# Output projection in four parts between attention steps, and bias adds moved behind the latest exp

## The chip, the cores and the metric

The kernel runs on one core of a Trainium2 chip. The core has engines with an instruction queue each: TensorE (PE, matrix products into PSUM), VectorE (DVE), ScalarE (ACT), GpSimd (POOL) and SyncE (SP, which issues the DMAs). Instructions of one engine run in their order; an instruction that needs another engine's result waits on a semaphore, and everything behind it in its queue waits too. The metric is the device time in microseconds, the median of several runs.

## The reference

Four layers on x of shape (4, 512, 32, 32) in float32, with 1024 tokens in each of four batches:

```
layer 0: attention, 8 heads of 64:   x = softmax(q k / 8) v @ Wo + bo + x
layer 1: linear attention:           x = x + gamma * wval(x)
layer 2: layer norm, one head of 512, x = x + out
layer 3: group norm, 4 heads of 128: x = x + proj(softmax(q k / sqrt(128)) v)
```

The change lies in the attention of layers 0 and 3, and in the code that forms q and k.

## The kernel before

Tokens are handled in two blocks of 512 (qb), channels in four chunks of 128 (g or o). `attention` serves layers 0 and 3. It goes through steps (qb, g, i). `scores` forms one product of keys and queries into a two-bank PSUM tile and takes its exp on ACT (L917) into a tile pt, which DVE adds to a running sum (L921, L924). `values` multiplies pt with v two steps later (L936 in layer 0, L951 in layer 3). In layer 0 a head is 64 wide and a chunk holds a pair of heads: the products there use 64 x 64 parts of the array, with four products to a step, and the loop takes two steps at a time (`per` is 2). In layer 3 a head is a chunk, products are 128 x 128, and `per` is 1.

When a chunk's steps are done, `sum_rows` (L963 or L971, and in layer 0 a copy on ACT at L968 and an add on DVE at L969) and `invert` (a reciprocal, L673, and two maxima, L675 and L676) give the softmax's divisor. `normalise` multiplies (L980) and adds the output bias to x in place, on ACT (L982).

When all four chunks of a block are done, `project_out` multiplies the attention's output (the tile ot) with the output weights. It uses seven products on 2 x 2 blocks in place of eight: product 1 in two halves, then 6, 7 and 5, then the second halves of 7 and 5, each of four matmuls of 128 x 256 (L1012). DVE forms the sums of inputs (`sum_inputs`, L681 to L684) and adds the results into x (L1020, L1041). The function is in two parts: `lead` holds the first half of product 1, a copy on ACT (L1032) and the input sums; `rest` holds all else. In layer 3 each finished piece is sent out by a DMA on SP (L1025). The fourth block of layer 0's last batch goes through `project_out_plain`, and the last block of layer 3 through `end_program`.

PSUM has four one-bank tiles (acc), which values, row sums, projections and the products of q and k share, and two two-bank tiles (sc), which scores use.

The order on PE is written out by hand (`manual_schedule`). Work that is to come later stands in a list, `later`, with a count that `tick` lowers; `tick` is called after each `values`, and an entry runs when its count is spent. The last block of a batch has its projection left in `later` when the next batch begins; there `seven_products`, which forms q and k, takes entries from the list between its first eight products (p1 and p2, L701): one after the fifth, all that is left after the sixth. Other engines' orders come from a scheduler that builds the program; `issue_after(ins)` holds the instructions traced inside it behind `ins` in their engine's queue.

Between the batches of layer 0, `pieces` of layer 1 for the batch before run in `slot`: the first, `gates`, takes a maximum over x on DVE (L1217) and four row sums on ACT (L1220).

Of the kernel before, what the change touches and what calls it, by code (L numbers as in the profile page):

```python
# [14 lines left out]
AF = mybir.ActivationFunctionType  # L15
# [459 lines left out]
def plain_path(ctx: ExitStack, tc: tile.TileContext, d: dict, out: bass.AP, count):  # L475
# [178 lines left out]
    def slot():  # L654
        tick()
        if pieces:
            pieces.pop(0)()
# [47 lines left out]
    def seven_products(  # L705
        n, weights, inputs, bias, dst, sums, ws=None, matmul=tokens_moving, view=lambda ps: ps,
        slots=0, first=False, done=lambda tb, o: None,
    ):

        stt = nc.vector.scalar_tensor_tensor
        one, five, seven, made = {}, {}, {}, {}  # L720
        inner = lambda o: block_sums(lambda i, j: weights(i, j, o))

        def mult(o, ps, w, x, start=True, stop=True, ms=(0, 1)):
            for m in ms:
                matmul(ps, w, x, m, o, start and m == 0, stop and m == 1)

        def join(out, ps, i, o, other):

            if bias is None:
                nc.vector.tensor_tensor(out, view(ps), other, ALU.add)  # L730
            else:
                joined[:] = [stt(out, view(ps), bias(i, o), other, ALU.add, ALU.add).ins]

        def p1(o, ms=(0, 1)):
            if 0 in ms:
                one[o] = acc_tile()
            mult(o, one[o], weights(0, 0, o), inputs(0, 0), stop=False, ms=ms)
            if 1 in ms:
                nc.scalar.copy(dst(0, 1, o), view(one[o]))  # L739

        def p2(o, ms=(0, 1)):
            mult(o, one[o], weights(0, 1, o), inputs(1, 0), start=False, ms=ms)
            if 1 in ms and bias is None:
                nc.scalar.copy(dst(0, 0, o), view(one.pop(o)))
            elif 1 in ms:
                nc.scalar.activation(dst(0, 0, o), one.pop(o), AF.Identity, bias=bias(0, o))

        def p3(o):
            mult(o, five[o], made[o][3], inputs(1, 1), start=False)
            join(dst(0, 1, o), five.pop(o), 0, o, dst(0, 1, o))  # L750
            done(1, o)

        def p4(o):
            mult(o, seven[o], weights(1, 1, o), t[3], start=False)
            join(dst(1, 0, o), seven.pop(o), 1, o, dst(0, 1, o))
            done(0, o)

        def p5(o):
            five[o] = acc_tile()
            mult(o, five[o], made[o][0], t[0], stop=False)  # L760
            join(dst(1, 1, o), five[o], 1, o, dst(1, 1, o))

        def p6(o):
            ps = acc_tile()
            mult(o, ps, made[o][1], t[1])
            nc.vector.tensor_tensor(dst(0, 1, o), dst(0, 1, o), view(ps), ALU.add)

        def p7(o):
            seven[o] = acc_tile()
            mult(o, seven[o], made[o][2], t[2], stop=False)  # L770
            nc.vector.tensor_tensor(dst(1, 1, o), dst(0, 1, o), view(seven[o]), ALU.add)


        if first:
            for f in (p1, p2):
                for m in range(2):
                    for o in range(n):
                        f(o, (m,))
            for o in range(2):
                made[o] = inner(o)  # L780
            t = sums()
        else:
            calls = [(p1, 0), (p1, 1), (p2, 0), (p2, 1)]
            if n > 2:
                calls += [(p1, 2), (p1, 3), (p2, 2), (p2, 3)]
            for i, (f, o) in enumerate(calls):
                f(o)
                if i < 2:
                    made[o] = (ws or inner)(o)
                if i == 1:  # L790
                    tick()
                if i == 4 and later:
                    later.pop(0)[1]()
                if i == min(5, len(calls) - 1):
                    t = sums()
                    while later:
                        later.pop(0)[1]()
                if i % 2 and i // 2 >= len(calls) // 2 - slots:
                    slot()
        for a in range(0, n, 2):  # L800
            for o in (a, a + 1):
                if o not in made:
                    made[o] = (ws or inner)(o)
            order = [
                (p6, a), (p7, a), (p6, a + 1), (p5, a), (p4, a), (p7, a + 1), (p3, a), (p5, a + 1),
                (p4, a + 1), (p3, a + 1),
            ]
            for i, (f, o) in enumerate(order):
                f(o)
                if i % 2:  # L810
                    slot()
# [75 lines left out]
    def attention(b, q, key, v, heads, scale, wo, os, bo, hooks={}, last=False, end=None, plain=False):  # L887
# [9 lines left out]
        steps = [  # L897
            (qb, g, i) for qb in range(NTB) for g in range(NC) for i in range(nsteps)
        ]
        pts, accs, rds, outs, ots = {}, {}, {}, {}, {}  # L900
        half = lambda i: slice(i * P // 2, (i + 1) * P // 2)

        def scores(n):
            qb, g, i = steps[n]
            ps = two_tile("sc")
            if pair:
                for h, s in itertools.product(range(2), range(2)):
                    nc.tensor.matmul(  # L908
                        ps[half(h), s, :], lhsT=key(g, i)[half(s), half(h)],
                        rhs=q[qb][half(s), g, :], start=True, stop=True,  # L910
                    )
            for s in range(0 if pair else 2):
                nc.tensor.matmul(  # L913
                    ps[:, s, :], lhsT=key(g, 2 * i + s), rhs=q[qb][:, g, :], start=True, stop=True
                )
            pt = pt_tile("pt")
            nc.scalar.activation(pt, ps, AF.Exp, scale=scale)  # L917
            pts[n] = pt
            if i == 1:
                accs[qb, g] = acc = sum_tile("sum")  # L920
                nc.vector.tensor_tensor(acc, pts[n - 1], pt, ALU.add)  # L921
            elif i > 1:
                acc = accs[qb, g]
                nc.vector.tensor_tensor(acc, acc, pt, ALU.add)  # L924
            if i == nsteps - 1 and not pair:
                nc.vector.tensor_tensor(acc[:, 0, :], acc[:, 0, :], acc[:, 1, :], ALU.add)
# [48 lines left out]
        def normalise(qb, g):  # L975
            rd = rds.pop((qb, g))
            if g == 0 and not pair:
                ots[qb] = chunks_tile("ot", "ot")
            o = ots[qb][:, g, :]
            nc.vector.tensor_tensor(o, o if pair else outs.pop((qb, g))[0], rd, ALU.mult)  # L980
            xv = x[:, g, bass.ts(qb, TB)]
            nc.scalar.activation(xv, xv, AF.Identity, bias=bo[:, g : g + 1])  # L982

        def finish(qb, o, ps):
            xv = x[:, o, bass.ts(qb, TB)]
# [4 lines left out]
        def project_out(qb):  # L990
# [26 lines left out]
            def add(i, out, *others):  # L1017

                for a in (view(ps[i]), *others):
                    nc.vector.tensor_tensor(out, out, a, ALU.add)  # L1020
# [6 lines left out]
                        xv(i, tb),  # L1027
                    )

            def lead():  # L1030
                mult(1, w(0, 0), inputs(0, 0), stop=False)
                nc.scalar.copy(d, view(ps[1]))  # L1032
                sum_inputs(t, inputs)

            def rest():
                mult(1, w(0, 1), inputs(1, 0), start=False)
                finish(0, 0, 1, xv(0, 0))
                mult(6, os[1], t[1])
                add(6, d)
                mult(7, os[2], t[2], stop=False)  # L1040
                nc.vector.tensor_tensor(e, d, view(ps[7]), ALU.add)  # L1041
                mult(5, os[0], t[0], stop=False)
                finish(1, 1, 5, xv(1, 1), e)
                mult(7, w(1, 1), t[3], start=False)
                finish(1, 0, 7, xv(1, 0), d)
                mult(5, os[3], inputs(1, 1), start=False)
                finish(0, 1, 5, xv(0, 1), d)

            return lead, rest

        def start_out(qb, halves):
            halves.extend(project_out(qb))
            halves[0]()

        def project_out_plain(qb):
            ot = ots.pop(qb)
# [35 lines left out]
        for m in range(0, len(steps) + 2, per):  # L1092
# [3 lines left out]
            for n in range(m, m + per):  # L1096
                if n >= 2:
# [11 lines left out]
                    if n - 2 == len(steps) - 1 and end is not None:  # L1109
                        flush()  # L1110
                        end_program(qb)
                    elif final and g == NC - 1 and plain and qb == NTB - 1:
                        later.append([2 * per + 1, lambda qb=qb: project_out_plain(qb)])
                    elif final and g == NC - 1:
                        halves = []
                        later.append([2 * per, lambda qb=qb, p=halves: start_out(qb, p)])
                        later.append([2 * per + 1, lambda p=halves: p[1]()])
                if parts:
                    parts.pop(0)()
                if n in hooks:  # L1120
# [598 lines left out]
```

## Time and profile before

| what | value |
|---|---|
| median of 3 runs | 2520.86 us (2520.38 to 2520.89) |
| profiled execution | 2520.85 us |
| its span | 2518.9 us |
| mean granted TensorE clock | 0.999 |
| ACT busy in the span | 705.5 us (28%) |
| DVE busy in the span | 1608.0 us (64%) |

The profile is one execution. A line of the timeline has the start in us, the duration, the engine, the source line, the operation, the tile written and the tiles read with partitions and elements, the count merged into the line, and in brackets the idle time before it and what ended it. A matmul in float32 leaves two records, so "x8" stands for four matmuls. An ACT_TABLE_LOAD changes the set of functions that ACT can evaluate. The wait list gives, for an engine's line and what it waited for, the total in us, how often, and the longest.

### The profile page before, as it was taken

The page shows a single profiled execution, that of the slowest core. Times are in us where ns is not written, and L with a number is a line of the kernel's source. Part 1 is how long each engine was busy: PE and PEld are TensorE (multiplying, and loading weights), DVE is VectorE, ACT ScalarE, POOL GpSimd, SP SyncE. Part 2 cuts the span into 40 slices and gives each one's busy share as a digit, 9 for nine tenths or more (in the row PEclk, how much of TensorE's full clock was granted, in tenths as well). Part 3 has the DMA queues.
Part 4 walks back from the last instruction along what each step waited for, and adds up shares of the span by engine and source line. Part 5 has one row for each costly group of instructions (what it writes and reads, how often), then busy time and mean ns, then how long its engine had stood idle before and what let it go on. Part 6 is the DMA issues. An engine that isn't in the chain of part 4 may idle for free.

```text
span 2518.9 us, 24923 instructions
## 1 busy us (share of the span) xinstructions
PE 2488.8 (99%) x10266; PEld 1287.7 (51%) x10266; DVE 1608.0 (64%) x1815; ACT 705.5 (28%) x859; POOL 254.8 (10%) x240
## 2 busy tenths in 40 slices
PE   9999999999999999999999999999999999999999
PEld 4545544554455444544645446446556455555653
DVE  3788578758875888647275463644764763565465
ACT  1444254325431543221120211202320320321121
POOL 4001100110011001111203011021010001002000
PEclk9999999999999999999999999999999999999999
DMA  5000010001000301010001010110010000000000
GB/s 213 1 1 1 5 68 1 1 5 68 1 1 5 118 9 51 4 67 34 34 1 67 0 44 28 67 67 17 17 35 16 0 17 17 1 17 17 0 13 22
DMA packets 23303, 72.46 MB, mean 29 GB/s; under 512 B 1808, under 2 KB 9488, under 8 KB 21136
## 3 DMA queue, kind: packets, MB, share of 16 engines
q1 hardware_dynamic: 23184, 70.82, 7.7%
q8 instruction: 82, 1.34, 0.2%
q14 instruction: 37, 0.30, 0.0%
HBM read 44.60 MB, written 25.17 MB: 28 GB/s over the span
## 4 chain that ended last, share of the span: by engine, by line
PE 94%; DVE 4%; ACT 1%; issue 1%; DMA 0%; SPq 0%; DVEq 0%; ACTq 0%
PE acc L701 18%; PE acc L819 12%; PE acc L1165 9%; PE acc L951 9%; PE sc L913 9%; PE acc L936 8%; PE sc L908 8%; PE acc L826 7%; PE acc L1012 5%; PE acc L963 1%; PE feat L638 1%; PE acc L971 1%; DVE rd L673 1%; DVE sum L924 1%; PE acc L638 1%; PE acc L1257 1%
## 5 line engine op out<-in xcount | busy, mean ns | idle before, releaser
L917 ACT ACTIVATE pt<-sc 128x1024 f32<-128x1024 f32 x384 | 380.1, 1022 | 561.4 <-PE sc L913 374.8
L924 DVE TENSOR_TENSOR sum<-sum,pt 128x1024 f32<-128x1024 f32 x256 | 313.1, 1223 | 42.2 <-ACT pt L917 30.6
L936 PE MATMUL acc<-pt,v 64*64 64x512 f32 x2048 | 290.1, 590 | 0.0
L908 PE MATMUL sc<-q,k 64*64 64x512 f32 x2048 | 273.6, 591 | 4.1 <-ACT pt L917 4.1
L913 PE MATMUL sc<-q,k 128*128 128x512 f32 x512 | 240.1, 593 | 0.7 <-ACT pt L917 0.7
L951 PE MATMUL acc<-pt,v 128*128 128x512 f32 x512 | 239.9, 592 | 0.0
L689 POOL TENSOR_TENSOR ws<-wqkv 128x256 f32<-128x256 f32 (+1 forms) x40 | 40.8, 1019 | 1352.5 <-PE acc L963 555.8
L673 DVE RECIPROCAL rd<-acc 128x512 f32<-128x512 f32 x32 | 107.4, 3357 | 107.5 <-PE acc L971 107.5
L701 PE MATMUL acc<-t,ws 128*128 128x512 f32 x384 | 173.9, 593 | 0.0
L1165 PE MATMUL acc<-pt,v 128*128 128x512 f32 x384 | 170.2, 593 | 0.0
L936 PEld LDWEIGHTS acc<-pt,v 64*64 64x64 f32 x2048 | 104.6, 133 | 122.5 <-issue 99.2
L908 PEld LDWEIGHTS sc<-q,k 64*64 64x64 f32 x2048 | 101.5, 133 | 127.5 <-issue 95.5
L951 PEld LDWEIGHTS acc<-pt,v 128*128 128x128 f32 x512 | 97.3, 190 | 122.5 <-issue 121.5
L913 PEld LDWEIGHTS sc<-q,k 128*128 128x128 f32 x512 | 96.7, 190 | 115.6 <-issue 94.4
L1165 PEld LDWEIGHTS acc<-pt,v 128*128 128x128 f32 x384 | 72.8, 190 | 90.9 <-issue 89.2
L701 PEld LDWEIGHTS acc<-t,ws 128*128 128x128 f32 x384 | 72.5, 190 | 89.2 <-issue 89.0
L921 DVE TENSOR_TENSOR sum<-pt 128x1024 f32<-128x1024 f32 x64 | 76.7, 1198 | 49.1 <-ACT pt L917 49.1
L673 DVE RECIPROCAL rd<-rs 128x512 f32<-128x512 f32 x32 | 107.3, 3353 | 1.1
L730 DVE TENSOR_TENSOR v<-acc,v 128x512 f32<-128x512 f32 x72 | 49.7, 691 | 65.9 <-PE acc L819 65.7
L739 ACT COPY v<-acc 128x512 f32<-128x512 f32 x24 | 14.0, 584 | 273.4 <-PE acc L819 273.4
L819 PE MATMUL acc<-ws,t 128*128 128x256 f32 x384 | 87.3, 379 | 0.0
L1012 PE MATMUL acc<-oi,os 128*128 128x256 f32 x336 | 76.7, 381 | 10.7 <-DVE x L1020 10.7
(272 smaller groups left out, 3517.6 us busy)
## 6 DMA issues: line engine op xcount, KB each, us to landing
home<-x SPq DMA_DIRECT2D x8, 2048.0 KB, 6.3
x<-home SPq DMA_DIRECT2D x8, 2048.0 KB, 7.8
out<-x SPq DMA_DIRECT2D x32, 256.0 KB, 2.1
x<-in_x SPq DMA_DIRECT2D x3, 2048.0 KB, 17.0
wo<-in_wo SPq DMA_DIRECT2D x3, 1024.0 KB, 5.1
w<-in_w SPq DMA_DIRECT2D x1, 3072.0 KB, 17.7
wqkv<-in_wqkv SPq DMA_DIRECT2D x1, 3072.0 KB, 11.4
wqkv<-in_wqkv SPq DMA_DIRECT2D x2, 1024.0 KB, 9.7
```

Source lines behind the costliest of these rows:

```text
L673: nc.vector.reciprocal(rd, ps)
L701: nc.tensor.matmul(ps, lhsT=w[:, m, :], rhs=x[:, m, :], start=start, stop=stop, skip_group_check=True)
L819: nc.tensor.matmul(ps[:, bass.ts(r, C // 2)], lhsT=x[:, m, bass.ts(2 * o + r, P)], rhs=w[:, m, :], start=(start and r == 0), stop=stop, sk ...
L826: nc.tensor.matmul(ps, lhsT=x[:, m, bass.ts(o, P)], rhs=w[:, m, :], start=start, stop=stop, skip_group_check=True,)
L908: nc.tensor.matmul(ps[half(h), s, :], lhsT=key(g, i)[half(s), half(h)], rhs=q[qb][half(s), g, :], start=True, stop=True,)
L913: nc.tensor.matmul(ps[:, s, :], lhsT=key(g, 2 * i + s), rhs=q[qb][:, g, :], start=True, stop=True)
L917: nc.scalar.activation(pt, ps, AF.Exp, scale=scale)
L924: nc.vector.tensor_tensor(acc, acc, pt, ALU.add)
L936: nc.tensor.matmul(outs[qb, g][r][half(s), :], lhsT=v[i // 2][half(r), i % 2, g * P + s * hd : g * P + (s + 1) * hd], rhs=pt[half(r), s, : ...
L951: nc.tensor.matmul(outs[qb, g][0], lhsT=v[j // 2][:, j % 2, bass.ts(g, P)], rhs=pt[:, s, :], start=(j == 0), stop=(j == NT - 1),)
L1012: nc.tensor.matmul(ps[i][:, bass.ts(o, n)], lhsT=w[:, m, bass.ts(o, P)], rhs=t[:, m, :], start=(start and m + o == 0), stop=(stop and m == ...
L1165: nc.tensor.matmul(out, lhsT=v[j // 2][:, j % 2, bass.ts(m, P)], rhs=pts[j][:, qb, :], start=(i == 0), stop=(i == NT - 1),)
```

## The change

`project_out` now does the work of `lead` when it is called, and returns three parts: `second` (second half of product 1, product 6), `third` (first halves of 7 and 5) and `fourth` (second halves). They are entered in `later` with counts one, two and three above the first part's in layer 0, and one, one and two in layer 3. In `seven_products` one entry is taken after each of the fifth to eighth products, and what is left after them. In `normalise` the bias add on ACT is held behind the exp traced last. The arithmetic is the same.

```
-                if i == 4 and later:
+                if i >= 4 and later:
                     later.pop(0)[1]()
                 if i == min(5, len(calls) - 1):
                     t = sums()
-                    while later:
-                        later.pop(0)[1]()
                 if i % 2 and i // 2 >= len(calls) // 2 - slots:
                     slot()
+        while later:
+            later.pop(0)[1]()
...
-            nc.scalar.activation(pt, ps, AF.Exp, scale=scale)
+            exps.append(nc.scalar.activation(pt, ps, AF.Exp, scale=scale).ins)
...
-            nc.scalar.activation(xv, xv, AF.Identity, bias=bo[:, g : g + 1])
+            with tc.issue_after(exps[-1]):
+                nc.scalar.activation(xv, xv, AF.Identity, bias=bo[:, g : g + 1])
...
-            def lead():
-                mult(1, w(0, 0), inputs(0, 0), stop=False)
-                nc.scalar.copy(d, view(ps[1]))
-                sum_inputs(t, inputs)
-
-            def rest():
+            mult(1, w(0, 0), inputs(0, 0), stop=False)
+            nc.scalar.copy(d, view(ps[1]))
+            sum_inputs(t, inputs)
+
+            def second():
                 mult(1, w(0, 1), inputs(1, 0), start=False)
                 finish(0, 0, 1, xv(0, 0))
                 mult(6, os[1], t[1])
                 add(6, d)
+
+            def third():
                 mult(7, os[2], t[2], stop=False)
                 nc.vector.tensor_tensor(e, d, view(ps[7]), ALU.add)
                 mult(5, os[0], t[0], stop=False)
                 finish(1, 1, 5, xv(1, 1), e)
+
+            def fourth():
                 mult(7, w(1, 1), t[3], start=False)
                 finish(1, 0, 7, xv(1, 0), d)
                 mult(5, os[3], inputs(1, 1), start=False)
                 finish(0, 1, 5, xv(0, 1), d)
 
-            return lead, rest
+            return second, third, fourth
...
-                        halves = []
-                        later.append([2 * per, lambda qb=qb, p=halves: start_out(qb, p)])
-                        later.append([2 * per + 1, lambda p=halves: p[1]()])
+                        rest = []
+                        later.append(
+                            [2 * per, lambda qb=qb, rest=rest: rest.extend(project_out(qb))]
+                        )
+                        for i in (1, 2, 3) if pair else (1, 1, 2):
+                            later.append([2 * per + i, lambda rest=rest: rest.pop(0)()])
```

More of the change, by code (lines that the diff above doesn't have):

```diff
@@ L899, in attention @@
         ]
-        pts, accs, rds, outs, ots = {}, {}, {}, {}, {}
+        pts, accs, rds, outs, ots, exps = {}, {}, {}, {}, {}, []
         half = lambda i: slice(i * P // 2, (i + 1) * P // 2)
@@ L1047, in rest @@
                 finish(0, 1, 5, xv(0, 1), d)
-            return lead, rest
-        def start_out(qb, halves):
-            halves.extend(project_out(qb))
-            halves[0]()
+            return second, third, fourth
         def project_out_plain(qb):
```

## The prediction

> **What bounds the kernel now.** I read the busy shares first, then the list of who waited for whom on TensorE (PE), then the timeline around each of those waits.
>
> ```profile
> PE 2488.8 (99%) x10266; PEld 1287.7 (51%) x10266; DVE 1608.0 (64%) x1815; ACT 705.5 (28%) x859; POOL 254.8 (10%) x240
> ...
> PE acc L1012 <- DVE x L1020: 10.7, 7, 1.8
> ...
> PE sc L908 <- ACT pt L917: 4.1, 4, 1.3
> ```
>
> PE is busy for 2488.8 of 2518.9 us, so a change of order can only win from the 30 us of gaps. The wait list (total us, times, longest) names two that this change can touch: 10.7 us in which the output projection waits for VectorE (DVE), and 4.1 us in which scores wait for an exp. The timeline shows three kinds of place; matmul records come two to a matmul, so "x8" is four.
>
> Place A, the middle of a batch in layer 0 (four times, each with 1.75 or 1.76 us idle):
>
> ```profile
> 155.70 1.89 PE L1012 MATMUL acc<-oi,os 128*128 128x256 f32 x8
> 156.15 2.55 DVE L924 TENSOR_TENSOR sum<-sum,pt 128x1024 f32<-128x1024 f32 x2
> 158.62 0.68 DVE L1020 TENSOR_TENSOR x<-x,acc 128x512 f32<-128x512 f32 x1
> ...
> 159.35 3.72 PE L1012 MATMUL acc<-oi,os 128*128 128x256 f32 x16 [1.76 <-DVE x L1020]
> ...
> 162.91 1.89 PE L1012 MATMUL acc<-ot,wo 128*128 128x256 f32 x8
> ...
> 164.63 1.89 PE L1012 MATMUL acc<-ot,os 128*128 128x256 f32 x8
> ...
> 166.46 1.09 PE L936 MATMUL acc<-pt,v 64*64 64x512 f32 x8
> ```
>
> Product 7 takes the PSUM buffer of product 1, which DVE's add at 158.62 frees; that add stands behind two sum adds. Place B, a batch boundary in layer 0 (three times, 1.23 us):
>
> ```profile
> 229.11 1.89 PE L1012 MATMUL acc<-oi,os 128*128 128x256 f32 x8
> ...
> 230.36 1.22 DVE L684 TENSOR_TENSOR t<-x,t 128x1024 f32<-128x1024 f32 x1
> ...
> 231.49 0.68 DVE L1020 TENSOR_TENSOR x<-x,acc 128x512 f32<-128x512 f32 x1
> ...
> 232.23 3.72 PE L1012 MATMUL acc<-oi,os 128*128 128x256 f32 x16 [1.23 <-DVE x L1020]
> ...
> 235.78 1.89 PE L1012 MATMUL acc<-ot,wo 128*128 128x256 f32 x8
> ```
>
> Place E, the start of a batch's attention in layer 0: batches 1 to 3 (1.27 us idle), then batch 0 (0.28 us):
>
> ```profile
> 326.43 1.58 ACT L982 ACTIVATE x<-x,bo 128x512 f32<-128x512 f32 x2 [22.86 <-PE acc L819]
> 327.18 1.95 PE L908 MATMUL sc<-q,k 64*64 64x512 f32 x16
> ...
> 328.03 1.28 ACT L917 ACT_TABLE_LOAD   x1
> 329.32 1.94 ACT L917 ACTIVATE pt<-sc 128x1024 f32<-128x1024 f32 x2
> 330.40 2.00 PE L908 MATMUL sc<-q,k 64*64 64x512 f32 x16 [1.27 <-ACT pt L917]
> ```
>
> ```profile
> 80.00 1.95 PE L908 MATMUL sc<-q,k 64*64 64x512 f32 x16
> ...
> 81.16 1.94 ACT L917 ACTIVATE pt<-sc 128x1024 f32<-128x1024 f32 x2 [0.33 <-PE sc L908]
> 82.23 2.00 PE L908 MATMUL sc<-q,k 64*64 64x512 f32 x16 [0.28 <-ACT pt L917]
> ```
>
> Two bias adds sit on ScalarE (ACT) until the value projection has read x; the table load stands behind them, and the first exp behind the load. In batch 0, with no load there, the second group of scores starts 2.23 us after the first, otherwise 3.22.
>
> **The change, part by part.** No instruction is added or removed; the order of the built, not yet run, program shows what moves. SP and POOL keep their order.
>
> *Place A, x4.* Four value matmuls now stand between products 6 and 7, then product 7 and the first half of 5, a score group of eight and four value matmuls, the last two half-products, and the remaining values. DVE's order up to the add is unchanged and its rows follow each other without a gap from 139.56 to 159.30, so the add frees the buffer at the same time. PE reaches product 7 at 157.42 (155.70 + 1.72, the distance of the rows 162.91 and 164.63) + 0.11 for the change of tile shape + 0.86 for the values + 0.05 = 158.4, and still waits until 159.35: the stall shrinks, it does not go. Won: 0.86. Paid: one more visit to 64-row work between products. Such a visit costs in the rows here: leaving 0.11 (164.63 + 1.72 = 166.35 against 166.46), 0.05 in its first group, 0.11 on the return, 0.27; around the first part of the projection 0.37 (leaving took 0.20). The other new visit lies within the stall. Net 0.49 to 0.59; 4 x 0.54 = 2.2 us. Next in line there are the sum adds of the next head group: DVE's L921 now precedes the last four output adds, and waits for exps of the scores that now start at about 163.0, so it ends near 167.2; the output adds end near 170.8, and the value matmuls that need their buffers start at 171.8. Ends: 0 (the add comes later by the whole gain) and 4 x (2.04 - 0.54) = 6.0 (it is there when PE arrives; 2.04 is 159.35 - 157.42 plus 0.11 of slow restart).
>
> The Trainium skill, "TensorEngine Tiling (Array Packing)", Key Properties, says that changing the tiling mode drains TensorE, which speaks against eight new visits. The trace agrees that a switch costs something. If a drain were a whole matmul (0.59 us in the rows of L936) at each of the two switches, a visit would cost 1.18, place A would lose 4 x 0.32 and the sum below would be 6.2 us instead of 9.7; the gaps in the rows say 0.27 to 0.37, and I go by them.
>
> *Place B, x3.* Two projection matmuls (p2 of chunk 2, 1.72 us) now stand between products 6 and 7, two more (p2 of chunk 3) before the last half-products. DVE's add also moves ahead of its 1.22 us L684, so it ends near 231.1; PE asks for the buffer at 229.11 + 1.72 + 1.72 = 232.55. The loss was 232.23 - 230.83 = 1.40 plus 0.10 of slow restart (3.55 to the next row instead of 3.45): 3 x 1.5 = 4.5 us. Shapes here are all 128-row, and neighbouring groups show no switch cost (225.67 to 227.38 is 1.71). Behind it, the output adds end at about 242.7, some 1.4 us later, while PE is 1.5 us ahead; then come DVE's 4.42 us maximum over x and two joins, due to end at 249, and PE needs them at about 255 (256.40 before). ACT's four row sums and POOL's four weight sums (5.5 us, waiting for the last product's reading of ot) start 1 to 3.5 us later and are wanted over 10 us after. Ends: 0 and 4.5.
>
> *Place E, x3.* The bias adds now follow the latest exp, one per head group. The load, which waits for nothing in the program, then runs some 23 us earlier, after the value copies. What is left is batch 0's case: 3.22 - 2.23 = 0.99, x3 = 3.0 us. Other end: the load waits for the first scores; an exp could then start at 327.18 + 1.16 + 1.28 = 329.62, 0.3 later than now, -0.9 us. The first end is nearer: the load began at 328.03, before those scores could be seen (327.18 + 1.16 = 328.34).
>
> *Bias adds among the exps, 64 of them.* Each is 0.71 us, mostly in front of the copy of the row sums (L968), which now idles 0.62, 0.83, 1.48 or 1.06 us first. The copy comes at most 0.1 us late; next to wait are DVE's add and reciprocal, and the following exps come after another 1.15 us of idle. I take 0; bound -0.1 x 24 = -2.4 if DVE passes every tenth on, and not above 0.
>
> *Layer 3, seven projections.* No wait there before, so nothing to win. In the middle, a score group, the row sum and two value products come before the last two half-products; the row sum's buffer is handed on after the 3.36 us reciprocal, a 1.16 us add and a 0.68 us maximum, at about 2031.5 in the time of the first such rows after 2016.8, and PE wants it at 2033.2: 1.7 us to spare. The output DMAs of the last part leave up to 6 us later on SP; behind them stand the next projection's and, in the second batch, one load of x wanted a batch later. I take 0, which is also the bound above; below, if the handover came as late as it now looks early, -1.7 x 4 = -6.8.
>
> **Sum.** 2.2 + 4.5 + 3.0 = 9.7 us. The profiled run took 2520.85 us around its span of 2518.9, the median is 2520.86: 2511.2 us, span 2509.2.
>
> **Rivals.**
> 1. The stall at A only moves (DVE is nearly full in layer 0's attention: seven sum adds of 1.22 us and 6.7 of normalising rows, some overlapping, in the 14.5 to 14.8 us between the copies of one head group and the next). For: gapless rows before A, and the switch price if it is higher than read. Against: 5.6 us of DVE gaps between 159.9 and 170.4. A gives 0: 2513.4.
> 2. The load is held by the scores, E gives -0.9 instead of 3.0, the sum is 5.8: 2515.1. For: layer 3's first load does wait (1729.90, after the scores of 1727.94). Against: there a wait stands ahead of the load in the program, here only on the exp.
> 3. A new wait at B: the joins behind the 4.42 us maximum come later than PE needs, which takes the 4.5 back, the sum is 5.2: 2515.7. Against: the 6 us to spare worked out above.
> 4. Slower: bias adds in ACT's queue hold the row-sum copy and then the exps. Price 0.71 x 28 head groups = 19.9 us if nothing hid them, 2531; it decides from 0.35 us a group reaching PE. Against: the idle of 0.62 to 1.48 just named.
> 5. The change does nothing: excluded by the built order, in which the parts stand apart.
>
> **Chances.** Forecast 0.70, rival 1 0.10, rival 2 0.06, rival 3 0.07, rival 4 0.07. About 0.2%, 5.0 us, is what a measurement of this kernel can tell from no change. Forecast and rival 1 lie clearly beyond it, rivals 2 and 3 (5.8 and 5.2 us) just at it. Faster is 0.70 + 0.10 + half of 0.13, less 0.04 for the bounds of layer 3 and of the row-sum copies: 0.82. Same is the other half and the 0.04: 0.11. Slower is rival 4: 0.07. The low end, 2508.5, is where A yields 4.9 of the 6.0 open to it; the high end, 2516, takes in rivals 1 to 3 and leaves rival 4 and the worst of layer 3 out.
>
> **What would show it.** Right: "L1012 <- DVE x L1020" falls from 10.7 us in 7 to about 3.5 in 4, none at boundaries; "L908 <- ACT" falls to about 1.1; the table load comes long before the first scores. Wrong: a new PE wait for DVE's maximum over the row sums, for L766/L771 after a boundary, or ACT idle gone before L968.

## The result and the profile after

The changed kernel takes 2511.6 us (median of 7 runs, 2510.95 to 2512.2), the kernel before 2520.38 us (7 runs beside it, 2519.92 to 2520.92). That is 8.8 us less, a ratio of 0.9965 with a 95% interval of 0.9953 to 0.9976. The profiled execution took 2511.6 us around a span of 2509.5 us, at a granted clock of 1.0. In the changed kernel some lines have other numbers: the products are L1013, the output adds L1021 and L1043, the bias add L983; the copy of the projection is still L1032.

The busy times on the page of the changed kernel:

```profile
PE 2489.5 (99%) x10266; PEld 1286.6 (51%) x10266; DVE 1606.4 (64%) x1815; ACT 705.3 (28%) x859; POOL 255.2 (10%) x240
```

Every engine does what it did: PE is busy for 0.7 us more, and the part of the span in which it is not busy fell from 30.1 to 20.0 us. So all that was won was idle time of PE. Its wait list (total us, times, longest):

```profile
PE acc L701 <- DMA wqkv<-in_wqkv: 4.7, 1, 4.7
PE acc L1013 <- DVE x L1021: 3.0, 4, 0.7
PE acc L963 <- DVE ot L947: 1.2, 4, 0.6
PE sc L908 <- ACT pt L917: 1.1, 4, 0.3
```

The products' wait for the output add is down from 10.7 us in seven to 3.0 in four, the scores' wait for an exp from 4.1 to 1.1. The first line, the load at the start, is about the same in every kernel and varies by itself; the third is new by 0.3 us and comes up again below.

Place A, the middle of a batch, in the timeline (start, duration, engine, line, operation, tiles, records; in brackets idle before and its releaser; here and below, rows that the argument does not need are left out):

```profile
148.45 1.99 PE L1013 MATMUL acc<-ot,wo 128*128 128x256 f32 x8
154.94 1.89 PE L1013 MATMUL acc<-oi,os 128*128 128x256 f32 x8
155.39 2.55 DVE L924 TENSOR_TENSOR sum<-sum,pt 128x1024 f32<-128x1024 f32 x2
156.76 1.09 PE L936 MATMUL acc<-pt,v 64*64 64x512 f32 x8
157.86 0.68 DVE L1021 TENSOR_TENSOR x<-x,acc 128x512 f32<-128x512 f32 x1
158.59 3.72 PE L1013 MATMUL acc<-oi,os 128*128 128x256 f32 x16 [0.74 <-DVE x L1021]
162.25 1.95 PE L908 MATMUL sc<-q,k 64*64 64x512 f32 x16
164.01 1.04 PE L936 MATMUL acc<-pt,v 64*64 64x512 f32 x8
164.98 1.99 PE L1013 MATMUL acc<-ot,wo 128*128 128x256 f32 x8
166.81 1.89 PE L1013 MATMUL acc<-ot,os 128*128 128x256 f32 x8
172.12 1.04 PE L963 MATMUL acc<-sum,ones 64*64 64x512 f32 x8
```

Product 7 starts 3.65 us after product 6 (158.59 - 154.94), exactly as before (159.35 - 155.70). The four values at 156.76 run inside what was a stall of 1.76 us; 0.74 us of it are left, since DVE's add still stands behind the two sum adds at 155.39.

Place B, a batch boundary:

```profile
222.69 1.89 PE L1013 MATMUL acc<-ot,wo 128*128 128x256 f32 x8
227.86 1.89 PE L1013 MATMUL acc<-oi,os 128*128 128x256 f32 x8
229.11 0.68 DVE L1021 TENSOR_TENSOR x<-x,acc 128x512 f32<-128x512 f32 x1
229.59 1.88 PE L701 MATMUL acc<-x,wqkv 128*128 128x512 f32 x4
231.31 3.62 PE L1013 MATMUL acc<-oi,os 128*128 128x256 f32 x16
234.76 1.88 PE L701 MATMUL acc<-x,wqkv 128*128 128x512 f32 x4
236.48 1.89 PE L1013 MATMUL acc<-ot,wo 128*128 128x256 f32 x8
239.93 3.60 PE L701 MATMUL acc<-t,ws 128*128 128x512 f32 x8
```

There is no bracket left: the add is done at 229.79, and product 7 is asked for at 231.31. Place E, the start of batch 1's attention:

```profile
300.23 1.28 ACT L917 ACT_TABLE_LOAD   x1
324.45 1.95 PE L908 MATMUL sc<-q,k 64*64 64x512 f32 x16
325.60 1.94 ACT L917 ACTIVATE pt<-sc 128x1024 f32<-128x1024 f32 x2 [24.09 <-PE sc L908]
326.68 2.00 PE L908 MATMUL sc<-q,k 64*64 64x512 f32 x16 [0.28 <-ACT pt L917]
```

The table load runs 24 us ahead of the first scores, and the second group of scores starts 2.23 us after the first, no longer 3.22.

Distances inside one trace price the three places. The rows at which places A and B begin and end in the kernel before:

```profile
149.21 1.99 PE L1012 MATMUL acc<-ot,wo 128*128 128x256 f32 x8
173.37 1.04 PE L963 MATMUL acc<-sum,ones 64*64 64x512 f32 x8
223.94 1.89 PE L1012 MATMUL acc<-ot,wo 128*128 128x256 f32 x8
242.67 3.60 PE L701 MATMUL acc<-t,ws 128*128 128x512 f32 x8
```

From the first part of the projection to the next row sums (L963), place A took 149.21 to 173.37, 24.16 us; now 148.45 to 172.12, 23.67 us: 0.49 won, four times. From the first part to the next product 6 of q and k, place B took 18.73 us (223.94 to 242.67); now 17.24 (222.69 to 239.93): 1.49 won, three times. Place E won 0.99, three times. Unrounded, the sum is 1.96 + 4.47 + 2.97 = 9.40 us. That the spans differ by 9.4 too is chance. The two traces are already 0.75 us apart at the first row sums (98.65 and 97.90), which come before any of these places; at the last row sums of layer 0 they are 9.78 apart (965.18 and 955.40). So layer 0 won 9.03 us: 9.40 less 0.37 for a new wait at the row sums, told below. The medians say 8.8.

### The profile page after: what moved, and what is told of

It reads as the page before. It is cut to its first block, busy times and chain, and to the rows that moved or that the text cites. A ratio compares the mean times of both kernels' runs of the same rounds, so it can differ in the third digit from the quotient of the medians.

```text
span 2509.5 us, 24916 instructions
## 1 busy us (share of the span) xinstructions
PE 2489.5 (99%) x10266; PEld 1286.6 (51%) x10266; DVE 1606.4 (64%) x1815; ACT 705.3 (28%) x859; POOL 255.2 (10%) x240
## 4 chain that ended last, share of the span: by engine, by line
PE 96%; DVE 3%; issue 1%; ACT 0%; DMA 0%; SPq 0%; DVEq 0%; ACTq 0%
PE acc L701 19%; PE acc L819 12%; PE acc L1168 9%; PE acc L951 9%; PE sc L913 9%; PE sc L908 8%; PE acc L936 8%; PE acc L826 7%; PE acc L1013 6%; PE acc L963 1%; PE acc L971 1%; PE feat L638 1%; DVE sum L924 1%; PE acc L638 1%; DVE rd L673 1%; PE acc L1260 1%
## 5 line engine op out<-in xcount | busy, mean ns | idle before, releaser
L826 PE MATMUL acc<-q,ln 128*128 128x512 f32 x192 | 85.9, 593 | 0.8 <-DVE pts L730 0.8
```

The lines of the kernel that those rows point to most:

```text
L826: nc.tensor.matmul(ps, lhsT=x[:, m, bass.ts(o, P)], rhs=w[:, m, :], start=start, stop=stop, skip_group_check=True,)
```

## The experiments

The theory: the three places are separate, each gives back idle time of PE, and nothing else counts. The rivals: the bias adds act otherwise than through the table load, or hold the exps; a gain at one place depends on another; layer 3 costs something that the gains hide; the switches between 64-row and 128-row products cost more than the gaps in the rows say. Medians in the first four runs stand against 2520.17 us for the kernel before, which ran beside them, and in the next four against 2520.28.

**The bias adds alone.** In the kernel before:

```
+            exps.append(nc.scalar.activation(pt, ps, AF.Exp, scale=scale).ins)
...
+            with tc.issue_after(exps[-1]):
                 nc.scalar.activation(xv, xv, AF.Identity, bias=bo[:, g : g + 1])
```

> The kernel before with one thing of the change, the bias adds behind the latest exp. Theory (place E): the table load runs long before the first scores, the second group of scores starts 2.23 us after the first in batches 1 to 3 and not 3.22, so 3 x 0.99 = 3.0 us are won: about 2517.4 us against 2520.4, L908 <- ACT falls from 4.1 to about 1.1 us. Rival 2 (the load is held by the scores): 0.9 us lost, 2521.3. Rival 4 (bias adds hold the row-sum copies and the exps): at least 0.35 us for each of 28 head groups, 2530 or more. A gain of 6 us or more would mean that the bias adds had held back the exps elsewhere too.

Measured: 2517.51 us, 2.7 us less (ratio 0.999, 0.9981 to 0.9999). Its wait list:

```profile
PE acc L1013 <- DVE x L1021: 10.7, 7, 1.8
PE sc L908 <- ACT pt L917: 1.1, 4, 0.3
```

The start of batch 1's attention in its timeline:

```profile
301.44 1.28 ACT L917 ACT_TABLE_LOAD   x1
325.66 1.95 PE L908 MATMUL sc<-q,k 64*64 64x512 f32 x16
327.89 2.00 PE L908 MATMUL sc<-q,k 64*64 64x512 f32 x16 [0.29 <-ACT pt L917]
```

The seven waits of the projection are untouched, and the scores' wait is down to 1.1 us. The load runs at 301.44, and the first two score groups start 2.23 us apart. PE's matmuls stand in the same order in both kernels, so the two traces can be laid side by side: after the first row sums, the distance between them grows by 1.0 us at the second score group of batches 1, 2 and 3, and drifts by less than 0.1 us between them. So E is the table load and nothing else. That the bias adds would hold the exps (rival 4) or the scores the load (rival 2) has fallen.

**The four parts alone.** The changed kernel, with the bias adds back:

```
-            with tc.issue_after(exps[-1]):
-                nc.scalar.activation(xv, xv, AF.Identity, bias=bo[:, g : g + 1])
+            nc.scalar.activation(xv, xv, AF.Identity, bias=bo[:, g : g + 1])
```

> The changed kernel with the bias adds back in their place. Theory: places A and B win what they won in the changed kernel, 4 x 0.49 + 3 x 1.49 = 6.4 us, and E nothing: about 2514.0 us; L908 <- ACT stays at 4.1 us. If the two halves of the change depend on each other (the bias adds delay the copies that the projection waits for), A or B falls short and the time lies above 2515.

Measured: 2513.73 us, 6.4 us less (0.9975, 0.9965 to 0.9984). The scores' wait is 4.1 us as before, that for the output add 2.9 us in four. The two halves of the change add up, 6.4 + 2.7 = 9.1 against 8.8 for both, within the scatter of the runs.

**Only the boundary.** As the last one, with the three later parts together inside a batch:

```
-                        for i in (1, 2, 3) if pair else (1, 1, 2):
+                        for i in (1, 1, 1):
```

> Only the boundary: the entries are still taken one by one between the products of q and k, but inside a batch the three later parts run together as before, and the bias adds stay in place. Theory (place B): 3 x 1.49 = 4.5 us, about 2515.9 us; the boundaries vanish from L1020's waits, the four waits of 1.76 us in the middle stay (7.0 us in 4). Rival (B is only won because A's work lies elsewhere): less than 2 us.

Measured: 2516.2 us, 4.0 us less (0.9983, 0.9974 to 0.9992). Its wait list has only the middles left:

```profile
PE acc L1012 <- DVE x L1020: 7.0, 4, 1.8
PE sc L908 <- ACT pt L917: 4.1, 4, 1.3
```

From the first part to the next product 6 it is 17.23 us (223.27 to 240.50), 1.50 less than before. The rows say 4.5, the medians 4.0; the executions of one kernel here lie up to 2.5 us apart, so the rows are the better price. From the first to the last row sums of layer 0 the trace gains 4.6 us on the kernel before.

**Only the middle.** The parts apart in the middle of layer 0's batches, `seven_products` as before, the bias adds in place:

```
-                if i >= 4 and later:
+                if i == 4 and later:
                     later.pop(0)[1]()
                 if i == min(5, len(calls) - 1):
                     t = sums()
+                    while later:
+                        later.pop(0)[1]()
...
-                        for i in (1, 2, 3) if pair else (1, 1, 2):
+                        for i in (1, 2, 3) if pair else (1, 1, 1):
```

> Only the middle of layer 0's batches: the later parts run at steps one, two and three there, at the boundary all that is left runs after the sixth product as before, in layer 3 together as before, and the bias adds stay in place. Theory (place A): 4 x 0.49 = 2.0 us, about 2518.4 us, which is the 1.76 us wait reduced to 0.74 and some 0.5 us for each more visit to 64-row work; three boundary waits of 1.2 us stay. Rival 1 (A gives nothing): 2520.4. The three part runs add up to 2.0 + 4.5 + 3.0 = 9.5 us, the whole change's 8.8 and a little, if the places are independent.

Measured: 2518.07 us, 2.1 us less (0.9991, 0.9982 to 1.0: at the edge of what can be told). From the first part to the row sums it is 23.65 us (148.53 to 172.18), 0.51 less than before. The three parts of the change done singly sum to 2.7 + 4.0 + 2.1 = 8.8 us, which is the whole change's gain. They are independent, but for the 0.4 us at the row sums told below, which come only with the parts apart both in the middle and at the boundary. The expectation divided the gain as 1.02 us of wait less some 0.5 a visit. The price of a visit is less, see below.

**Layer 3 undivided.** The changed kernel, but in layer 3 one entry for the three later parts:

```
-                        for i in (1, 2, 3) if pair else (1, 1, 2):
-                            later.append([2 * per + i, lambda rest=rest: rest.pop(0)()])
+                        if pair:
+                            for i in (1, 2, 3):
+                                later.append([2 * per + i, lambda rest=rest: rest.pop(0)()])
+                        else:
+                            later.append([2 * per + 1, lambda rest=rest: [f() for f in rest]])
```

> The changed kernel, but in layer 3 the three later parts run together one step after the first, as before. Theory (layer 3 is worth nothing either way): within 0.5 us of the changed kernel, 2511.6. If the layer-3 split had cost something that the gains hid (bound 6.8 us), this kernel is faster than the changed one by that; if it had won something, slower.

Measured: 2510.99 us (5 runs, 2510.63 to 2513.1; 0.9963, 0.995 to 0.9976), 0.6 us below the changed kernel's 2511.6, a little more than the 0.5 expected, and inside its runs' scatter. The rows settle it: the first row sums of layer 3 begin at 1744.39 before and at 1734.32 in the changed kernel, the last at 2495.97 and 2485.89. The two are 10.07 and 10.08 us apart, so the seven projections between them won and cost nothing.

**The sum adds behind the output add.** In `project_out` of layer 0 the exp additions that are traced between the first and second part are put behind product 1's add (`finish` and `add` now return it), on the changed kernel:

```
+            elif i > 1 and held:
+                held[0].append((accs[qb, g], pt))
...
             sum_inputs(t, inputs)
+            if pair:
+                held.append([])
...
-                finish(0, 0, 1, xv(0, 0))
+                ins = finish(0, 0, 1, xv(0, 0))
+                for acc, pt in held.pop() if held else ():
+                    with tc.issue_after(ins):
+                        nc.vector.tensor_tensor(acc, acc, pt, ALU.add)
```

> The changed kernel, with the two additions of exps that stand in VectorE's queue ahead of the add of product 1 (2.55 us) put behind it, in the middle of layer 0's batches. Theory: the 0.74 us that product 7 still waits there is these two; the add then ends near 156.1 in the time of the first place, PE is there at 157.85, so the wait goes: 4 x 0.74 = 3.0 us and up to 0.1 each of slow restart, 2508.4 +- 0.4; L1021 vanishes from PE's waits. Rival (VectorE is full, the delay only goes to the next who needs it: the copies of outputs, the row sums): the gain is below 1 us and a wait for VectorE appears at L936 or L963.

Measured: 2507.35 us (0.9949, 0.9936 to 0.9963), 4.2 us below the changed kernel. Place A in its timeline:

```profile
154.59 1.89 PE L1016 MATMUL acc<-oi,os 128*128 128x256 f32 x8
155.03 0.68 DVE L1024 TENSOR_TENSOR x<-x,acc 128x512 f32<-128x512 f32 x1
155.63 1.22 DVE L1047 TENSOR_TENSOR sum<-sum,pt 128x1024 f32<-128x1024 f32 x1
156.41 1.09 PE L939 MATMUL acc<-pt,v 64*64 64x512 f32 x8
157.43 3.72 PE L1016 MATMUL acc<-oi,os 128*128 128x256 f32 x16
```

The add (L1024 here) starts at 155.03, as soon as the input sums are done, and product 7 follows the values without idle time. The place takes 22.85 us (148.10 to 170.95), 0.82 less than in the changed kernel: 0.74 of stall and 0.08 of slow restart. No wait for DVE took its place. 4 x 0.82 = 3.3 us of the 4.2; 0.4 more is that PE's wait at the row sums (L963) is 0.8 us in all and not 1.2. The expected 2508.4 +- 0.4 was missed by 0.65: it did not have this wait, and the 0.5 us that the rows leave over is within the scatter of the runs.

**The third part one step later.** On the changed kernel:

```
-                        for i in (1, 2, 3) if pair else (1, 1, 2):
+                        for i in (1, 3, 4) if pair else (1, 1, 2):
```

> The changed kernel with the third and fourth part one step of values later in layer 0, so that a score group stands between product 6 and product 7 and none between the third and the fourth part; as many visits to 64-row work. Theory: the 0.74 us of wait is covered by the 1.7 us of scores, 4 x 0.74 = 3.0 us, 2508.6. Rival: the last output adds, now some 1.5 to 2 us later, hold the buffers that the next head group's values take (1.0 us to spare in the changed kernel), and the wait comes back there: 2510 to 2513.

Measured: 2507.59 us (0.9951, 0.9937 to 0.9964), 1.0 below the 2508.6 expected; here too the row sums' wait is 0.8 and not 1.2 us. The place takes 22.85 us here too (147.95 to 170.80):

```profile
156.26 1.09 PE L936 MATMUL acc<-pt,v 64*64 64x512 f32 x8
157.17 1.90 PE L908 MATMUL sc<-q,k 64*64 64x512 f32 x16
158.88 1.04 PE L936 MATMUL acc<-pt,v 64*64 64x512 f32 x8
159.85 3.72 PE L1013 MATMUL acc<-oi,os 128*128 128x256 f32 x16
```

The stall can thus be covered from PE's side as well as taken away on DVE's. The later output adds held up nobody.

**One more cut.** The changed kernel with its third part cut between product 7 and product 5:

```
                 nc.vector.tensor_tensor(e, d, view(ps[7]), ALU.add)
+
+            def third_b():
                 mult(5, os[0], t[0], stop=False)
...
-            return second, third, fourth
+            return second, third, third_b, fourth
...
-                        for i in (1, 2, 3) if pair else (1, 1, 2):
+                        for i in (1, 2, 3, 4) if pair else (1, 1, 1, 2):
```

> The changed kernel with its third part cut once more, between product 7 and product 5: one more visit to 64-row work in each of the four places, and no wait expected for it. It prices what is disputed, the switch of the tile shape. By the gaps in the rows (0.27 to 0.37 a visit) 4 visits cost 1.1 to 1.5 us, 2512.7 to 2513.1; by a drain of a whole matmul at each switch (1.18 a visit) 4.7 us, 2516.3.

Measured: 2512.28 us (0.9969, 0.9957 to 0.9981), 0.7 above the changed kernel. In the timeline:

```profile
158.09 1.99 PE L1013 MATMUL acc<-oi,os 128*128 128x256 f32 x8 [0.74 <-DVE x L1021]
160.02 1.95 PE L908 MATMUL sc<-q,k 64*64 64x512 f32 x16
161.78 1.04 PE L936 MATMUL acc<-pt,v 64*64 64x512 f32 x8
162.75 1.99 PE L1013 MATMUL acc<-oi,os 128*128 128x256 f32 x8
```

The stall is the same 0.74 us, and the place takes 24.02 us (147.95 to 171.97), 0.35 more than in the changed kernel, for one more visit to 64-row work. Four make 1.4 us; the row sums' wait gives 0.4 back (0.8 for 1.2). That is 1.0 us, and the median, 0.4 below the expected 2512.7 to 2513.1, says 0.7. A drain of a whole matmul at each switch, 1.18 us a visit, is excluded.

**Taking away the stall and the visits.** The sum adds behind the output add, and inside a batch the later parts together as in the kernel before; beside it the same with layer 3 undivided too, and the changed kernel once more. On the version with the sum adds behind:

```
-                        for i in (1, 2, 3) if pair else (1, 1, 2):
+                        for i in (1, 1, 1) if pair else (1, 1, 2):
```

> The changed kernel with the two additions of exps behind the add of product 1, and the three later parts run together inside a layer-0 batch, as in the kernel before (at the boundary and in layer 3 the parts stay apart). If the wait in the middle is those additions alone, product 7 follows product 6 at once with nothing between them, and the two more visits to 64-row work are saved: from 2507.35 by 4 x 0.37 to 4 x 0.53, which is 1.5 to 2.1 us, to 2505.2 to 2505.9. From the start of the projection to the next row sums the first place then takes about 22.3 to 22.5 us (24.16 before, 23.67 changed, 22.85 with the additions behind). Rival (without other work in between VectorE falls behind inside the projection): the wait comes back at the second half of product 7 for L1053's read of it, and the time is 2507 or more.

> The same, with layer 3's three later parts together as well: only the boundaries of layer 0 and 3 and the bias adds are left of the change. Theory: layer 3 is worth nothing, within 0.6 us of the kernel with the parts apart there, either way.

> The changed kernel itself, beside the two others on the same chip: 2511.6 us, from which the others are to differ by about 6 us.

Measured on one chip: 2504.2 us (0.9937, 0.9924 to 0.9951), with layer 3 undivided 2504.72 (0.9939, 0.9926 to 0.9953), the changed kernel 2511.58 (0.9966, 0.9952 to 0.9979), the kernel before 2520.22. The first of them in the timeline:

```profile
155.70 5.34 PE L1016 MATMUL acc<-oi,os 128*128 128x256 f32 x24
156.14 0.68 DVE L1024 TENSOR_TENSOR x<-x,acc 128x512 f32<-128x512 f32 x1
156.74 1.22 DVE L1047 TENSOR_TENSOR sum<-sum,pt 128x1024 f32<-128x1024 f32 x1
157.87 0.68 DVE L1024 TENSOR_TENSOR ou<-ou,acc 128x512 f32<-128x512 f32 x1
158.47 1.22 DVE L1047 TENSOR_TENSOR sum<-sum,pt 128x1024 f32<-128x1024 f32 x1
159.60 0.68 DVE L1053 TENSOR_TENSOR ou<-ou,acc 128x512 f32<-128x512 f32 x1
160.88 1.89 PE L1016 MATMUL acc<-ot,wo 128*128 128x256 f32 x8
```

Products 6, 7 and the first half of 5 now run as one row of 24 records. DVE's read of product 7 (L1053) ends at 160.28, 0.6 us before PE adds to that buffer at 160.88, so the rival's wait does not come. The place takes 22.13 us (149.21 to 171.34): 0.72 less than with the parts apart, 2.03 less than before. Two visits are saved, 0.36 each. The expectation had them too cheap at 0.37 to 0.53 for both, and 2504.2 lies 1.0 below its 2505.2 to 2505.9. The best kernel seen keeps the change at the boundaries, in layer 3 and for the bias adds, and in the middle undoes it in favour of an order on DVE: 16.0 us below the kernel before and 7.4 below the changed one, where about 6 had been expected.

## Why the prediction was right, and where it was off

The forecast was 2511.2 us with a span of 2509.2; measured are 2511.6 and 2509.5, and the mechanisms are those named. That the times agree within 0.4 us is partly luck: the gain was forecast as 9.7 us and measured as 8.8, and the forecast started from 2520.86, while the kernel before took 2520.38 beside the changed one.

- **Place A** (0.86 - 0.27 to 0.37, taken as 0.54, 2.2 us): 0.49 a place by the rows, 2.0 us, and 2.1 by the run that has it alone. The mechanism was told rightly: DVE's order up to the add is unchanged, so product 7 starts no earlier, and values move into the stall. The term that was a little off is the visit. Product 7 to the scores takes 3.66 us (158.59 to 162.25) against 3.56 before, the scores 1.76 against 1.71, the values 0.97 against 0.86, and the next half-product 1.83 against 1.72: 0.10 + 0.05 + 0.11 + 0.11 = 0.37. The 0.27 had left out the last of these, the slow first group after the return. The other visit, in the stall, cost nothing, as was said. That 2.04 us lay there was seen too: the upper end, 6.0, is four times this less 0.54, for an add that is there when PE arrives. In the two kernels where it is there and the parts stay apart, the place gave 1.31 (24.16 - 22.85), 5.2 us, since two visits cost 0.72. What was not seen is that the add can be there with no visit paid: with two sum adds moved and the later parts together, the place gives 2.03 a time, 8.1 us. Rival 1 has fallen as it stood, since A gave its 2.0; the 0.37 us at the row sums, below, is all that may have moved. (Its room on DVE was a little larger than it says: the copies of successive head groups are 14.5 to 15.5 us apart, 96.36, 110.90, 125.70 and 141.15 in the rows of L946.)
- **Place B** (4.5 us): 1.49 three times, 4.5 by the rows; 4.0 by the medians of the run that has it alone. The wait behind DVE's maximum (rival 3) has no entry in the list of waits.
- **Place E** (3.0 us): 0.99 three times; 2.7 by the medians of the bias adds alone. The load's not waiting, argued from a start 0.3 us too early for it, was shown.
- **Bias adds among the exps** (0): most row-sum copies still have idle time of ACT before them (0.46 us at 144.27, 1.06 before), but before eight of the 32 it is gone, which the prediction gave as a sign of being wrong. It cost nothing: such a copy starts 1.08 us after its row sums (172.12 to 173.20) and 1.09 in the kernel before (173.37 to 174.46). So ACT's idle time going is no sign of a loss as long as the copy is not late.
- **Layer 3** (0): nothing by the rows, and by medians two comparisons that differ in sign (2510.99 against 2511.6, and 2504.72 against 2504.2).
- **The switch of the tile shape.** By the Trainium skill, "TensorEngine Tiling (Array Packing)", Key Properties, a change of tiling mode drains TensorE. The runs agree that it costs: 0.35, 0.36 and 0.37 us a visit, from three comparisons. It is far from two whole matmuls. Whether the cost is a drain, no run here shows.
- **The sum**: 9.7 us forecast, 9.4 by the rows of the places, 9.0 with the wait at the row sums, 8.8 by medians. Of the 0.3 to the rows of the places, 0.2 is place A. A wait that the forecast does not have is 0.57 us at the row sums of layer 0's last batch (879.10), where before the longest was 0.2 us. It came in all three kernels that have the parts apart both in the middle and at the boundary and A's stall of 0.74 us as it was; with one more cut, and in all other kernels, it did not come. It follows a DVE idle of 0.46 us at 874.76, before a sum add that waits for an exp, though the exp begins no later than before (873.43 against 883.09, 9.66 apart like the rows around them). The cause stays open. What can be told from no change was set too high at 5.0 us: the bias adds alone, 2.7 us, have an interval of 0.9981 to 0.9999.

## What to carry to other kernels

Where TensorE waits for a buffer, look first at what stands ahead of the releasing instruction in the other engine's queue: here two additions that nobody was waiting for were worth 2.03 us a place; work pushed between the products gave 0.49, and 1.31 where there was enough of it to cover the stall. Putting other work into a stall hides the stall but pays for every change of tile shape once the stall is gone, so it is best with work of the same shape, as at the boundary. An instruction that changes an engine's state, like a table load, can be hidden for nothing if what stands ahead of it in its queue needs no late data.

## What the runs showed of the hardware

- A visit of 64-row work between 128-row products costs about 0.36 us, in four pieces: 0.10 on leaving, 0.05 in the first 64-row group, 0.11 on the return and 0.11 in the first 128-row group after it. Between 128-row products of different kinds there is none of it (boundary: 227.86, 229.59, 231.31 are 1.73 and 1.72 apart).
- An ACT table load of 1.28 us, free of late data ahead of it, ran 24 us before the exp that needs it, and the exp after the scores then started without any further delay (scores at 324.45, exp at 325.60, 1.15 later; in batch 0, without a load, 1.16).
- The wait for the first load of weights is 4.3 to 5.7 us in the single executions profiled here, whatever the kernel, and the first row sums, before any place of the change, begin between 97.17 and 99.45 us. Distances between rows of one trace repeat within 0.02 us (place A: 23.66 or 23.67 four times), so effects below 1 us are read from them, not from two spans.
